# The attention projections of a two-layer kernel as Strassen products over heads, batches and halves of the inputs

## The chip, the cores and the metric

The kernel runs on one core of one Trainium2 chip. A core has five engines that run beside each other and wait for each other by semaphores: PE (TensorE, matmuls; its weight loads are listed as PEld), DVE (VectorE), ACT (ScalarE), POOL (GpSimd) and SP (SyncE, which here only issues DMA transfers). Matmuls read SBUF and write PSUM, which has eight banks of 2 KB per partition. The metric is the device time of one execution in microseconds. Before the change it is 3163.42 us, the median of three runs (3163.29 to 3165.45).

## The reference

Two layers, each an attention-like part times a gated MLP, added to the input; all in float32. Of the first layer, which the change is in:

```python
xn = _layernorm(x, axis=-1)                       # x: 2 x 1024 x 512
q = silu(causal_dwconv(xn @ Wq, qcw, qcb))        # Wq, Wk, Wv, Wg: 512 x 2048, 16 heads of 128
k = silu(causal_dwconv(xn @ Wk, kcw, kcb))        # convolution over 4 tokens
v = silu(causal_dwconv(xn @ Wv, vcw, vcb))
def step(S, ...):                                 # over 1024 tokens, per batch and head
    err = S @ kt - vt
    S = at * S - bt * outer(err, kt)
    ot = S @ qt
o = layernorm(o over the head) * ln_w + ln_b
s = (o * sigmoid(xn @ Wg)) @ Wo
x = x + s * silu(mlp(xn))
```

The second layer has a gated linear recurrence and an MLP with 4-bit weights; the change does not touch its work.

## The kernel before

**Front (0 to 393 us).** x is normalised, transposed and kept in SBUF as `xnT` (128 x 4 x 2 x 1024: input part, batch, token). The first layer's MLP runs step by step on PE; between its steps (`some`, L455) the kernel makes k of head groups 0 to 2 (`for hg in range(3)`, L987). A head group is two heads of both batches, four streams; there are eight groups. k is written to DRAM, as are the decay factors e and the inverses of triangular blocks (`invert`, L746) that the recurrence needs.

**The loop (393 to 1814 us).** The recurrence is done in chunks of 128 tokens. A round u of the loop (L1122) handles one group and one chunk; two groups take turns, so there are 64 rounds of some 22 us, and four rounds cover a window of 256 tokens of two groups. In a round stand `within` (L785, products of one chunk: pk, pqk), `across` (L832, the recurrent chain: pks, pr, zw, pst, with its state), `finish` (L907, output, normalisation, gate), and beside them two pieces of projection. A piece is one of q, k, v, gate for one group and one window. `wide` (L608) makes it: for each of two heads, four matmuls of 512 columns (256 tokens of two batches) over the four parts of the inputs, into one PSUM bank:

```python
lhsT=w[:, kc, hl * P : (hl + 1) * P],
rhs=xnT[:, kc, :, p * 2 * P : (p + 1) * 2 * P],
```

`project` (L624) then copies the sum out (ACT), makes the convolution's last tap out of PSUM (ACT), the other three taps (DVE, six instructions a piece), and silu (ACT). `gated` (L676) takes tanh straight from PSUM. POOL copies the margins of three tokens from window to window (`halo`) and makes kg, qg, rs and the gated output. k of groups 3 to 7 is made in the loop, one piece in each of two rounds of four, followed by `ahead_l` (L725, product pkk).

**Order.** In the loop PE, DVE, ACT and POOL keep the order in which the program records their instructions (`Ordered`, L124). `weave` (L1040) divides a round into ten slots, advances one link of one of two chains in each, and shares out the other products by planned costs. `later(n, ...)` (L593) records a step n slots on; a sum that PE has just finished is thus evicted in the next slot. SP's transfers are in-order on SP's queue: among them the 12 small copies of a round that regroup w into wt (`back`, L876), ground, kb, eb, eg, od. A late instruction on one of these queues delays all behind it.

**PSUM in the loop.** Pool "a" has three banks (pieces, pqk, pkk, half outputs), "i" one (pk), "s" one, "o" one, "z" two.

**After the loop.** `Join` (L140) multiplies the outputs by Wo for each of 16 tiles of 128 tokens, multiplies by the MLP's result, adds x, normalises and transposes for the second layer. For eight tiles (`pd`) the half of the product over the first eight heads is made in late rounds of the loop (`half`) and parked in DRAM. Wo is loaded in rounds 58 to 61 (`load_wo`).

Of the kernel before, what the change touches and what calls it, by code (L numbers as in the profile page):

```python
# [13 lines left out]
F32 = mybir.dt.float32  # L14
# [125 lines left out]
class Join:  # L140
# [5 lines left out]
    def __init__(self, tc, a, cst, minus_half, od, gd, x1d, pd):  # L146
        self.tc, self.a, self.cst, self.minus_half = tc, a, cst, minus_half
        self.od, self.gd, self.x1d, self.pd, self.a = od, gd, x1d, pd, a
        self.ctx = ExitStack()
        self.tp = [self.pool("j_t", 1)]  # L150
        self.wp, self.op = self.pool("j_w", 1), [self.pool("j_o", 1)]
        self.lp = self.pool("j_ln", 3)
        self.wo = []
        self.order = [(c, b) for c in range(NC) for b in range(B)]
        self.o, self.xg, self.made = [], [], 0
        self.load_xg()
# [4 lines left out]
    def load_wo(self):  # L161

        h0 = len(self.wo)
        w = self.wp.tile([P, 4, D], F32, name=f"wo_{h0}")
        self.tc.nc.sync.dma_start(
            w, self.a["wo"][h0 * P : (h0 + 4) * P, :].rearrange("(h p) e -> p h e", p=P)
        )
        self.wo += [w[:, h, :] for h in range(4)]
# [139 lines left out]
def first_layer(ctx, tc, a, cst, minus_half, keep, xnT, od, gd, pd, then):  # L308
# [34 lines left out]
    kp = early.enter_context(tc.tile_pool(name="at_k", bufs=1))  # L343
    dr = ctx.enter_context(tc.tile_pool(name="at_d", bufs=6, space=DRAM))
# [14 lines left out]
    pools["p"] = front.enter_context(  # L359
        tc.tile_pool(name="f0_p", bufs=3, side="right", reuse_waits="tile")  # L360
    )
# [139 lines left out]

    cw = cp.tile([P, 3, H, 4], F32, name="cw")
# [12 lines left out]
    def load_weights(hg, names, queue=nc.sync):  # L515
        w = {}
        for n in names:
            pool = pools["w"] if n != "wk" else kp if "b" in pools or not hg else fz
            w[n] = pool.tile([P, KC, 2 * P], F32, tag=n, name=f"{n}_{hg}")
            queue.dma_start(  # L520
                w[n], a[n][:, hg * 256 : (hg + 1) * 256].rearrange("(kc p) n -> p kc n", p=P)
            )
        return w


# [82 lines left out]
    def wide(name, hg, p, w):  # L608


        for hl in range(2):
            pool, tag = (pools["i"], "pi") if "b" not in pools and hl else (pools["a"], "pa")
            pp = pool.tile([P, B, 2 * P], F32, tag=tag, name=f"{name}_{hl}")
            for kc in range(KC):
                mm(
                    pp,
                    lhsT=w[:, kc, hl * P : (hl + 1) * P],
                    rhs=xnT[:, kc, :, p * 2 * P : (p + 1) * 2 * P],
                    start=(kc == 0),
                    stop=(kc == KC - 1),  # L620
                )
                yield WIDE, (hl, pp) if kc == KC - 1 else None

    def project(j, n, hg, p, w, dst):  # L624

        u = f"{n}_{hg}_{p}"

        def convolved(hl, pp):
            h = hg * 2 + hl
            pre = pools["p"].tile([P, B, 2 * P + 4], F32, tag="pre", name=f"pre{u}_{hl}", bufs=3)  # L630
            acc = dst[:, 2 * hl : 2 * hl + 2, :]

            def first():
                if p == 0:
                    POOL.memset(pre[:, :, 0:3], 0.0)
                else:
                    POOL.tensor_copy(pre[:, :, 0:3], halo[:, j, h % 4, :, 0:3])
                ACT.copy(pre[:, :, 3 : 2 * P + 3], pp)
                ACT.activation(
                    acc, pp, AF.Identity, scale=cw[:, j, h, 3:4], bias=cb[:, j, h : h + 1]  # L640
                )

            def taps(*which):
                for tap in which:
                    DVE.scalar_tensor_tensor(
                        acc,
                        in0=pre[:, :, tap : tap + 2 * P],
                        scalar=cw[:, j, h, tap : tap + 1],
                        in1=acc,
                        op0=ALU.mult,  # L650
                        op1=ALU.add,
                    )

            def second():
                if p < NC // 2 - 1:
                    POOL.tensor_copy(halo[:, j, h % 4, :, 0:3], pre[:, :, 2 * P : 2 * P + 3])
                taps(0, 1)

            def fourth():
                if hl:  # L660
                    ACT.activation(dst, dst, AF.Silu)

            if j == 2 and hg >= HG - 3 and hl:

                later(1, first, lambda: (second(), taps(2)), fourth)
            elif j == 2 and hg >= HG - 3:
                later(1, lambda: (first(), second()), lambda: (taps(2), fourth()))
            else:
                later(1, first, second, lambda: taps(2), fourth)

        for cost, ready in wide(f"p{u}", hg, p, w):
            if ready:
                convolved(*ready)
            yield cost

    def gated(hg, p, w, gate):  # L676
        def act(part, pg):

            ACT.activation(part, pg, AF.Tanh, scale=0.5)
            ACT.activation(part, part, AF.Identity, bias=1.0)  # L680

        for cost, ready in wide(f"pgate_{hg}_{p}", hg, p, w):
            if ready:
                hl, pg = ready
                later(1, functools.partial(act, gate[:, 2 * hl : 2 * hl + 2, :], pg))
            yield cost


    def ahead_k(hg, p, wk, store):
        ka = pa.tile([P, NS, 2 * P], F32, tag="ka", name=f"ka_{hg}_{p}")  # L690
        store["ka", p] = ka
        yield from project(1, "wk", hg, p, wk, ka)
        later(5, lambda: nc.sync.dma_start(store["k"][p], ka))
# [31 lines left out]
    def ahead_l(hg, c, store):  # L725
# [3 lines left out]
        pool, tag = (pools["a"], "pa") if order["loop"] else (pools["i"], "pi")  # L729
        pkk = pool.tile([P, NS, P], F32, tag=tag, name=f"pkk_{hg}_{c}")  # L730
# [54 lines left out]
    def within(hg, c, store):  # L785
# [3 lines left out]
        q = windows[hg, c // 2]["q"][:, :, half]  # L789
# [8 lines left out]
        def block(s):  # L798
# [14 lines left out]
            lambda: POOL.tensor_tensor(qg, q, eg[:, :, 1 : P + 1], ALU.mult),  # L813
# [10 lines left out]
        pqk = pools["a"].tile([P, NS, P], F32, tag="pa", name=f"pqk_{u}")  # L824
# [7 lines left out]
    def across(hg, c):  # L832
# [9 lines left out]
        vv = windows[hg, c // 2]["v"][:, :, half].rearrange("p s (b t) -> p s b t", t=32)  # L842
# [64 lines left out]
    def finish(hg, c):  # L907
# [46 lines left out]
        gate = windows[hg, c // 2]["gate"][:, :, half]  # L954

        def gate_it():
            POOL.tensor_tensor(ot, ot, gate, ALU.mult)
# [20 lines left out]
    def ell():  # L978
        if ls:
            hg, p = ls.pop(0)  # L980
            for c in (2 * p, 2 * p + 1):
                done(ahead_l(hg, c, stores[hg]))
                if c == 2 * p:
                    some(1)

    of_e = ()
    for hg in range(3):  # L987
        stores[hg] = new_store(hg)
        wk = load_weights(hg, ("wk",))
        steps = invert(hg - 1, stores[hg - 1]) if hg else iter(())  # L990
        for p in range(NP):
# [3 lines left out]
            done(ahead_k(hg, p, wk["wk"], stores[hg]))  # L995
# [18 lines left out]
    for n, bufs, at in (("g", 1, ctx), ("b", 2, ctx), ("w", 2, last_w)):  # L1014
# [7 lines left out]
    for n, bufs in (("a", 3), ("i", 1), ("s", 1), ("o", 1), ("z", 2)):  # L1022
# [5 lines left out]
    def made(hg, p, n):  # L1028

        dst = pools["b"].tile([P, NS, 2 * P], F32, tag=n, name=f"{n}_{hg}_{p}")  # L1030
# [733 lines left out]
```

## Time and profile before

| | us |
|---|---|
| median of three runs | 3163.42 |
| span of the profiled execution | 3161.9 |
| PE busy | 3135.2 (99%) |
| DVE busy | 2149.5 (68%) |
| ACT busy | 1253.1 (40%) |
| POOL busy | 826.8 (26%) |
| front / loop / joining / second layer | 392.6 / 1421.7 / 144.8 / 1202.8 |

The profile is of one execution, a few tenths of a per cent at most from the others. A row of a group reads: line, engine, operation, tiles written <- read, shapes, count | busy us, mean ns of one | idle time before. Most rows have line 132, the helper that records the instructions; so groups are told apart by their tiles. A float32 matmul leaves two records, each 0.16 us longer than the step to the next one, since matmuls are pipelined; its cost is therefore taken from start to start.

### The profile page before, as it was taken

The page shows a single profiled execution, that of the slowest core. Times are in us where ns is not written, and L with a number is a line of the kernel's source. Part 1 is how long each engine was busy: PE and PEld are TensorE (multiplying, and loading weights), DVE is VectorE, ACT ScalarE, POOL GpSimd, SP SyncE. Part 2 cuts the span into 40 slices and gives each one's busy share as a digit, 9 for nine tenths or more (in the row PEclk, how much of TensorE's full clock was granted, in tenths as well). Part 3 has the DMA queues.
Part 4 walks back from the last instruction along what each step waited for, and adds up shares of the span by engine and source line. Part 5 has one row for each costly group of instructions (what it writes and reads, how often), then busy time and mean ns, then how long its engine had stood idle before and what let it go on. Part 6 is the DMA issues. An engine that isn't in the chain of part 4 may idle for free.

```text
span 3161.9 us, 38109 instructions
## 1 busy us (share of the span) xinstructions
PE 3135.2 (99%) x12390; PEld 1942.6 (61%) x12390; DVE 2149.5 (68%) x4294; ACT 1253.1 (40%) x2269; POOL 826.8 (26%) x1210
## 2 busy tenths in 40 slices
PE   8999999999999999999999999999999999999998
PEld 7577756666666666666666644555555555555554
DVE  4557678786877878675554455677767666776677
ACT  3476555546555555544333211222222222222223
POOL 2000123223222222322222211333333333333322
PEclk9999999999999999999999999999999999999999
DMA  6244344444444443444324465000101001010014
GB/s 184 63 120 112 102 137 119 109 133 124 126 108 127 140 127 105 107 142 106 89 82 144 118 206 154 29 27 27 33 28 34 27 27 34 27 34 27 27 37 133
DMA packets 499750, 287.40 MB, mean 91 GB/s; under 512 B 207584, under 2 KB 440800, under 8 KB 499552
## 3 DMA queue, kind: packets, MB, share of 16 engines
q1 hardware_dynamic: 490688, 268.97, 30.2%
q0 software_dynamic: 6560, 11.80, 1.3%
q10 hardware_dynamic: 2304, 4.20, 0.4%
q8 instruction: 99, 1.62, 0.2%
q14 instruction: 99, 0.81, 0.1%
HBM read 183.90 MB, written 88.34 MB: 86 GB/s over the span
## 4 chain that ended last, share of the span: by engine, by line
PE 92%; DVE 4%; ACT 1%; issue 1%; DMA 1%; SPq 0%; POOL 0%; DVEq 0%; ACTq 0%; POOLq 0%
PE po L132 18%; PE pua L132 7%; PE pga L132 7%; PE pgate L132 6%; PE pwq L132 6%; PE pwv L132 6%; PE pwk L132 6%; PE zw L132 4%; PE jpo L211 4%; PE puc L132 3%; PE pgc L132 3%; PE pu L132 3%; PE pg L132 3%; PE pr L132 2%; PE pub L132 2%; PE pgb L132 2%
## 5 line engine op out<-in xcount | busy, mean ns | idle before, releaser
L132 DVE TENSOR_TENSOR acc<-acc,po 128x512 f32<-128x512 f32 x408 | 278.1, 682 | 208.4 <-PE po L132 207.7
L132 PEld LDWEIGHTS po<-w_d,i 128*128 128x128 f32 x1024 | 194.5, 190 | 142.6 <-issue 110.7
L132 PE MATMUL po<-w_d,i 128*128 128x256 f32 (+1 forms) x1024 | 275.3, 392 | 0.0
L132 PE MATMUL pgate<-xnT,wg 128*128 128x512 f32 x512 | 245.7, 593 | 0.0
L132 PE MATMUL pwq<-xnT,wq 128*128 128x512 f32 x512 | 245.2, 593 | 0.0
L132 PE MATMUL pwv<-xnT,wv 128*128 128x512 f32 x512 | 243.0, 593 | 1.8 <-ACT gate L132 1.8
L132 PE MATMUL pua<-xq,w_u 128*128 128x512 f32 x512 | 240.6, 592 | 0.0
L132 PE MATMUL pga<-xq,w_g 128*128 128x512 f32 x512 | 240.6, 592 | 0.0
L132 PE MATMUL pwk<-xnT,wk 128*128 128x512 f32 x512 | 236.1, 593 | 1.3 <-ACT ka L132 1.3
L132 ACT COPY g<-pga 128x512 f32<-128x512 f32 x96 | 56.3, 586 | 445.8 <-PE pga L132 438.4
L132 ACT COPY w<-zw 128x128 f32<-128x128 f32 x192 | 50.8, 265 | 368.3 <-PE zw L132 368.2
L132 PEld LDWEIGHTS po<-w_d,s 128*128 128x128 f32 x720 | 136.8, 190 | 95.4 <-issue 77.0
L132 DVE SCALAR_TENSOR_TENSOR v<-prewv,cw,v 128x512 f32<-128x512 f32 x192 | 165.3, 861 | 43.6 <-ACT v L132 35.3
L132 DVE TENSOR_TENSOR rr<-rr,zw 128x128 f32<-128x128 f32 x192 | 54.8, 286 | 205.0 <-PE zw L132 201.4
L132 PE MATMUL po<-w_d,s 128*128 128x256 f32 x720 | 184.8, 379 | 0.0
L132 POOL TENSOR_TENSOR rs<-rs,minus_half 128x4 f32<-128x4 f32 x64 | 64.5, 1008 | 433.1 <-DVE rs L132 415.2
L132 ACT ACT_TABLE_LOAD x133 | 170.6, 1283 | 17.8 <-PE pr L132 11.3
L132 POOL TENSOR_TENSOR ot<-ot,gate 128x512 f32<-128x512 f32 x64 | 85.7, 1340 | 350.2 <-ACT ot L132 320.5
L132 PEld LDWEIGHTS zw<-rr,ground 128*128 128x128 f32 x512 | 97.0, 191 | 122.1 <-issue 102.4
L132 DVE SCALAR_TENSOR_TENSOR ka<-prewk,cw,ka 128x512 f32<-128x512 f32 x192 | 147.7, 771 | 30.2 <-ACT ka L132 25.3
L132 DVE SCALAR_TENSOR_TENSOR q<-prewq,cw,q 128x512 f32<-128x512 f32 x192 | 158.0, 824 | 12.2 <-POOL eg L132 7.0
L132 PEld LDWEIGHTS zw<-w,ground 128*128 128x128 f32 x768 | 110.9, 191 | 64.1 <-issue 53.7
(248 smaller groups left out, 6645.7 us busy)
## 6 DMA issues: line engine op xcount, KB each, us to landing
e<-gr SPq DMA_DIRECT2D x64, 256.0 KB, 4.1
de<-e SPq DMA_DIRECT2D x64, 256.0 KB, 2.7
dk<-ka SPq DMA_DIRECT2D x32, 512.0 KB, 2.8
kb<-dk SPq DMA_DIRECT2D x64, 256.0 KB, 3.4
eg<-egr SPq DMA_DIRECT2D x64, 256.0 KB, 4.0
eb<-de SPq DMA_DIRECT2D x64, 256.0 KB, 3.4
od<-ot SPq DMA_DIRECT2D x64, 256.0 KB, 2.2
wt<-w SPq DMA_DIRECT2D x768, 16.0 KB, 1.9
```

The costliest lines, as they stand in the source:

```text
L132: i = getattr(self.engine, name)(*args, **kw)
L211: matmul(po, lhsT=ot[:, h, :], rhs=self.wo[h], start=(h == h0), stop=(h == H - 1))
```

## The change

A piece is no longer a plain product. It is seen as a product of 2 x 2 blocks: two heads (rows), two halves of the 512 inputs (inner), two batches (columns). By Strassen's scheme in Winograd's form the eight block products become seven; each is two matmuls of 256 columns (`quarter`), 14 for a piece. The operands are sums: three weight blocks and three x blocks more, plus two changed in place, so a set is seven blocks.

- x sums: made once per window in the front by POOL (`x_sums`) and written to DRAM (`dx`); in the loop the seven blocks of a window are loaded into the room of `xnT` itself (`load_x`, two windows at a time; `boths` has the rest of that room), every fourth round.
- weight sums: for each weight and group made once by POOL after loading (`load_w`, p = 0), written to DRAM (`dw`) and reloaded for each further window. Four buffers of a set; two sets are loaded each round.
- a piece (`Piece.step`): products 0, 5, 6, 3 add up in one bank (A), which ACT copies out after each; products 1 and 4 go to a second bank (X), from which one ACT copy takes both; product 2 adds to X, and DVE adds it out of PSUM. POOL (before round 48) or DVE adds the pair to the outer quarters. Then come convolution and silu, or tanh, out of SBUF, in more slots than before. The copy that fed the convolution's last tap from PSUM is replaced by one from SBUF.
- two pieces of a round are interleaved in a fixed order of steps (`ORDER`, `woven`), and the pieces of the four turns are redistributed (`tasks`): k and gate; v and k; q and gate; q and v.
- PSUM: "a" has two banks, "x" one; pkk and pqk move to "i", which has one.
- k of group 3 moves to the front, where k pieces are made with plain products (`direct`); the loop makes k of groups 4 to 7. The first q and v pieces of groups 0 and 1 are made ahead of the loop, with their loads and sums on POOL's queue.
- eleven halves of the output product instead of eight (`pd`); Wo goes to xnT's room in round 62.

Core of the diff:

```diff
-    def wide(name, hg, p, w):
-        for hl in range(2):
-            pool, tag = (pools["i"], "pi") if "b" not in pools and hl else (pools["a"], "pa")
-            pp = pool.tile([P, B, 2 * P], F32, tag=tag, name=f"{name}_{hl}")
-            for kc in range(KC):
-                mm(pp, lhsT=w[:, kc, hl * P : (hl + 1) * P],
-                    rhs=xnT[:, kc, :, p * 2 * P : (p + 1) * 2 * P], ...)
+    def quarter(out, w, x, i, first):
+        for kc in range(2):
+            mm(out, lhsT=w[:, i, kc, :], rhs=x[:, i, kc, :],
+                start=(first and kc == 0), stop=(kc == 1), skip_group_check=not first)
...
+        def step(self, i):
+            out = self.out
+            if i in (0, 5, 6, 3):
+                for step in self.of_a:
+                    step()
+                self.of_a = []
+                quarter(self.A, self.w, self.x, i, i == 0)
+                at = {0: 0, 5: 1, 6: 3, 3: 2}[i]
+                def copied():
+                    ACT.copy(out[:, at], self.A)
+                    ...
+                self.evicted(self.of_a, copied)
+            elif i == 1:
+                self.X = pools["x"].tile([P, 2, 2 * P], F32, tag="X", name=f"px{self.u}")
+                quarter(self.X[:, 0], self.w, self.x, 1, True)
+            elif i == 4:
+                quarter(self.X[:, 1], self.w, self.x, 4, True)
+                def pair():
+                    ACT.copy(self.both, self.X)
+                    self.end()
+                self.evicted(self.of_x, pair)
+            else:
+                for step in self.of_x:
+                    step()
+                quarter(self.X[:, 1], self.w, self.x, 2, False)
+                def add():
+                    DVE.tensor_tensor(out[:, 1], out[:, 1], self.X[:, 1], ALU.add)
+                    self.ended()
+                later(1, add)
...
-        pkk = pool.tile([P, NS, P], F32, tag=tag, name=f"pkk_{hg}_{c}")
+        pkk = pools["i"].tile([P, NS, P], F32, tag="pi", name=f"pkk_{hg}_{c}")
...
-        pqk = pools["a"].tile([P, NS, P], F32, tag="pa", name=f"pqk_{u}")
+        pqk = pools["i"].tile([P, NS, P], F32, tag="pi", name=f"pqk_{u}")
...
-    for hg in range(3):
+    for hg in range(4):
...
-    for n, bufs in (("a", 3), ("i", 1), ("s", 1), ("o", 1), ("z", 2)):
+    for n, bufs in (("a", 2), ("x", 1), ("i", 1), ("s", 1), ("o", 1), ("z", 2)):
...
+    def load_w(n, hg, p, queue):
+        w = pools["w"].tile([P, 7, 2, P], F32, tag="w", name=f"w{n}_{hg}_{p}")
+        if p:
+            return [
+                lambda: queue.dma_start(w[:, 0:4], dw[n, hg][:, 0:4]),
+                lambda: queue.dma_start(w[:, 4:7], dw[n, hg][:, 4:7]),
+            ], [], []
+        ...
+            lambda: POOL.tensor_tensor(s1, a21, a22, ALU.add),
+            lambda: POOL.tensor_tensor(s2, s1, a11, ALU.subtract),
+            lambda: POOL.tensor_tensor(s4, a12, s2, ALU.subtract),
+            lambda: POOL.tensor_tensor(a21, a11, a21, ALU.subtract),
+        ], [lambda: queue.dma_start(dw[n, hg], w)]
...
+    ORDER = (
+        (0, 0), (1, 0), (0, 1), (0, 4), (0, 5), (1, 5), (0, 2),
+        (0, 6), (1, 6), (1, 1), (1, 4), (0, 3), (1, 3), (1, 2),
+    )
...
+            for i, t in enumerate(tasks(u + 1)):
+                loads, sums, kept = load_w(*t, nc.sync)
+                later(2 + 2 * i, *loads)
+                later(5 + 2 * i, lambda sums=sums: [step() for step in sums])
+                later(9, *kept)
+            if turn4 == 3 and u // 4 + 2 < 4 * NP:
+                later(1, *load_x(u // 4 + 2, nc.sync))
...
-    pd = {i: tc.dram_tile([P, D], F32, name=f"pd_{i}") for i in (4, 5, 7, 8, 10, 11, 12, 13)}
+    pd = {i: tc.dram_tile([P, D], F32, name=f"pd_{i}") for i in range(3, 14)}
```

## The prediction

> **What bounds the kernel now.** I read the page first, then the busy time by stage, the chain and PE's waits, then eight rounds of the loop, and last single rows. Part 1 and the chain of the page:
>
> ```profile
> PE 3135.2 (99%) x12390; PEld 1942.6 (61%) x12390; DVE 2149.5 (68%) x4294; ACT 1253.1 (40%) x2269; POOL 826.8 (26%) x1210
> PE 92%; DVE 4%; ACT 1%; issue 1%; DMA 1%; SPq 0%; POOL 0%; DVEq 0%; ACTq 0%; POOLq 0%
> ```
>
> TensorE is busy 99% and is 92% of the chain: only 27 us of the span are not matmuls. So work taken from PE is time gained, as long as nothing else becomes late. PE's waits inside the loop say how late the others are now (PE's waits, 392.6 to 1814.3 us):
>
> ```profile
> PE pst L132 <- DVE wt L132: 1.9, 2, 1.7
> PE pwv L132 <- ACT gate L132: 1.8, 3, 0.6
> PE zw L132 <- ACT w L132: 1.7, 5, 0.5
> ```
>
> A few us in 1422: nothing is late. The stages (front, rounds up to 32, later rounds, joining, second layer), then single rounds; columns are stretch, length, busy us of PE, PEld, DVE, ACT, POOL, clock, DMA share, GB/s:
>
> ```profile
> 392.60:1149.20 756.60, 753.93 (x3591) 484.05 (x3591) 579.23 (x1359) 417.09 (x832) 205.72 (x396) 1.00 0.46 125
> 1149.20:1814.30 665.10, 660.81 (x3194) 429.58 (x3193) 409.02 (x1073) 284.61 (x596) 173.79 (x273) 1.00 0.41 112
> ...
> 449.80:472.60 22.80, 22.80 (x115) 15.00 (x114) 19.85 (x47) 11.92 (x23) 5.55 (x12) 1.00 0.36 103
> 472.60:496.50 23.90, 23.31 (x116) 15.22 (x115) 19.06 (x44) 14.65 (x31) 7.40 (x13) 1.00 0.37 98
> 496.50:519.10 22.60, 22.23 (x106) 14.04 (x105) 21.53 (x51) 9.83 (x20) 6.44 (x15) 1.00 0.35 93
> 519.10:541.10 22.00, 22.00 (x107) 14.02 (x107) 18.55 (x48) 12.21 (x27) 7.10 (x13) 1.00 0.38 116
> ```
>
> The second engine is DVE: 79.0 us in these four rounds of 91.3. In the round where it is at 95% PE already lost 0.4 us. The clock is 1.00, so it plays no part.
>
> **The change part by part.** *Products.* A piece (one of q, k, v, gate for two heads and 256 tokens of both batches) is 8 matmuls of 512 columns now and 14 of 256 afterwards. A matmul has two records here. What 256 columns cost is seen in the second layer (PE's timeline):
>
> ```profile
> 2205.09 1.02 PE L132 MATMUL puc<-xq,w_u 128*128 128x512 f32 x2
> 2205.95 1.03 PE L132 MATMUL po<-w_d,s 128*128 128x256 f32 x4
> 2206.81 1.02 PE L132 MATMUL pga<-xq,w_g 128*128 128x512 f32 x2
> ```
>
> From start to start one matmul of 512 columns takes 0.86 us and two of 256 take 0.86: half the columns are half the time, with a new weight load each. A piece goes from 6.88 to 6.02 us. Of 128 pieces 112 change (the 16 k pieces of head groups 0 to 3 are made in the front in the old way): 112 x 0.86 = **-96.3 us**, all on the path.
>
> *Moved.* k of group 3 goes from loop to front, and three more half output products (11 for 8) from the joining into late rounds; the same matmuls, 0. Cover: DVE in the front is 239 of 393 us, in the late rounds 409 of 665. If the cover were gone, four k pieces' taps (24 x 0.77 us) would be the cost.
>
> *Transition to the loop.* Now PE runs from the front into the first product without a gap (PE's timeline at 392.63 us). Afterwards the x sums are read back into xnT's own room, so 7 of 14 loads must wait for the last direct k matmul, on POOL's queue. About 12 us of PE work stand between (21 records of the MLP's last product at 0.235, three pkk at 0.9, more). Behind the waiting load on POOL are six weight loads, the 3.3 us clearing of the ground, and 16 weight sums before the first four pieces, 8 more before round 0. POOL's issue row is 0.75 us; a 128x256 sum takes 0.79 to 0.83; so a weight set costs POOL 2 x 0.75 + 4 x 0.8 + 0.75 = 5.5 us against 6.0 of PE, plus landings of 6.7 us. I work out that PE stands some 3 us for wk's and 2 for gate's sums, and put 2 for the start: **+7**. Ends: 0 (all covered) and 25 (the loads of 1.8 MB land one behind the other, as uwT and dwT did at 9 and 11.4 us).
>
> *DVE.* Each piece adds one add of 128x256 out of PSUM; neighbours are 286 ns (128x128, rr) and 682 ns (128x512, kd), I take 0.42. POOL gets a 128x512 add per piece (its rows are 1.27 to 1.40 us) while the round is below 48. POOL's work slows DVE's taps: 137 of v's 192 taps meet no POOL tensor instruction and take 749 ns, the nine wholly beneath one take 1268 on average. In the trace:
>
> ```profile
> 507.11 2.45 DVE L132 SCALAR_TENSOR_TENSOR v<-prewv,cw,v 128x512 f32<-128x512 f32 x2
> ...
> 507.29 1.73 POOL L132 TENSOR_TENSOR kg<-kb,eg 128x512 f32<-128x512 f32 x1
> ```
>
> Two taps that take 1.5 us alone took 2.45. Summed over q, v, ka and the inversion's tl and ml this excess is 73 us, against 310 us of POOL's large work: 0.24 us per us. Per round POOL gains 2 x 1.34, so DVE gains 0.64 + 0.84. Four rounds: 79.0 + 3.4 + 2.6 = 85.0, against PE's 91.3 - 6.9 = 84.4. DVE is then as full as PE. Worse, the new order puts v and k pieces in one round (turn 1), whose 12 taps fall mostly in one stretch: I count 24.7 us of DVE in rounds 1, 9, 17, 25 against PE's 21.1, and 17.5 in the next. Late next: the add that frees the single X bank, and kd, lt, at, which now share one PSUM bank (pi) where three banks served; PE returns to it about 3.8 us later, so about 1 us of lateness is free. 2.6 us in such a round and 1.4 in round 3 of 8: **+16** over four such eights. Ends: 0 (the order's slack covers 3.6 us) and 60 (DVE late in every one of the 32 rounds by 2).
>
> [...]
>
> *ACT.* A piece's evictions become four copies of 128x256 and one of 128x512, from two of 128x512; the scaled copy then reads SBUF. Rows: 265 ns at 128x128, 586 at 128x512, I take 0.40: +1.0 us for q, k, v, and +1.8 for gate (two of 128x1024 at 1.06 for four of 0.62). The instruction order of the changed kernel has 38 more table loads, all in rounds up to 30, because tanh, silu and exp now alternate more:
>
> ```profile
> L132 ACT ACT_TABLE_LOAD x32 | 41.1, 1283 | 0.5
> ```
>
> 38 x 1.283 = 49 us of ACT, 1.5 per round. The fullest rounds (5, 13, ..) come to 20.9 of 22: covered, 0, with at most the 0.6 us of the longest ACT wait now at each such round.
>
> [...]
>
> *Queues.* SP issues 26 transfers a round at 0.55 us, 14.3 us. Added are four weight loads per round (0.42 to 0.46 each) and seven of x sums every fourth: by rows the two rounds after these hold 43 to 45 us of issues in 42. Behind them wait the wt copies (12 a round), needed some 10 us after their slot and landing in 1.9. The bytes: 2 x 0.92 + 0.46 MB a round are 109 GB/s beside 125 at a share of 0.46; at the same rate the share becomes 0.86. On 12 rounds POOL carries 3.2 or 6.4 us of weight sums and waits for their landing, ahead of kg and rs. I put **+10** for these; ends 0 and 40 (3 us in 13 rounds).
>
> *Joining.* Half products follow each other eleven times, where four did; there the DMA share was 0.95 at 288 GB/s, and 4 MB of wo move into rounds 62 and 63. **+2**, ends 0 and 15.
>
> Sum: -96.3 + 7 + 16 + 10 + 2 = -61.3. The profiled execution's span is 3161.9 us; 3100.6 follows. The median of the three runs, 3163.4, lies 1.5 above that span, so I say **3102**.
>
> **The rivals.** *All is covered.* PE's waits now are 6 us in the loop, which speaks for it; DVE at 85.0 of 84.4 against it. 3163.4 - 96.3 + 2 to 12 = 3069 to 3080.
>
> *DVE or SP becomes the bound of the first 32 rounds.* For: the sums above, where both reach PE's new time. Against: the late half has room (61%). With DVE's and the queues' ends, 60 + 40, most of the gain is gone: 3125 to 3157.
>
> *Slower: PE stands at each hand-over of the accumulating bank.* The new piece returns to bank A three times and to X once while ACT must first copy the earlier sum, and DVE frees X: five hand-overs a piece, where there were two with a bank to spare. At 0.17 us each, 112 x 5 x 0.17 = 96, the gain is gone; at 0.3 it is 3163 + 72 = 3235. Now such a wait reaches 0.6 us, in three cases. Against it: two or more other steps, 2 to 3 us, lie between the returns, and a copy takes 0.4.
>
> **How the numbers follow.** My forecast (3080 to 3125) 0.52; all covered 0.16; bound of DVE or SP 0.20; slower 0.10; no difference beyond 0.2% (6 us, about what a measurement of this kernel can tell) 0.02. Faster 0.88, same 0.02, slower 0.10. The range leaves out the slower case and the ends of the others: 3072 to 3145.
>
> **What would show it.** Right: rows of 14 x 2 records of 128x256 per piece, and PE's busy time near 3040; rounds 2 to 32 of about 21 us, with waits of PE on DVE (kd, lt, at, X's add) in every eighth round, few beyond round 32; a gap of 5 to 10 us near 420 us. Wrong: waits of PE on ACT's copies out of bank A in most rounds, 256-column matmuls further apart than 0.43 us, or SP's transfers landing so late that PE waits for wt or G.

## The result and the profile after

The changed kernel takes 3376.57 us (median; 3373.87 to 3379.14) beside 3164.28 us before (four runs made beside it): a ratio of 1.0673, 95% interval 1.0658 to 1.0688. It is 212 us slower; 61 us faster was forecast, and the time lies far outside the range. The direction is that of the third rival, to which the forecast gave 0.10, but not for its reason, as will be seen.

Part 1 of the page after, its row of granted clock and the chain:

```profile
PE 3132.9 (93%) x13734; PEld 2245.8 (67%) x13734; DVE 2207.3 (65%) x4429; ACT 1416.7 (42%) x2646; POOL 1051.3 (31%) x1304
...
PEclk9999989999889999999999999999999999999999
...
PE 37%; DVE 0%; DMA 0%; issue 0%; POOL 0%; ACT 0%; SPq 0%; ACTq 0%; DVEq 0%; POOLq 0%
```

PE's busy time is the same as before (3132.9, was 3135.2), although 95 us of matmuls were taken out. Busy time counts a matmul at half clock as nearly twice as long (four records of 128x256 took 1.92 us at 665.64 us, where the clock was 0.50, and 1.03 at 656.60, where it was 1.00), so the saving has been eaten inside the busy time as well; the 8s in the clock's row say where. The chain can't be followed through the loop any more, so the waits have to be read instead. PE's waits in the loop (523 to 2010 us), in total, times, longest:

```profile
PE pk L132 <- DMA kb<-dk: 61.9, 18, 7.7
PE pqk L132 <- DVE kd L132: 58.9, 34, 4.6
PE pxq L132 <- ACT xnT L132: 16.3, 9, 3.2
PE paq L132 <- ACT preq L132: 12.6, 12, 3.1
PE pak L132 <- ACT prek L132: 12.1, 6, 3.7
PE pkk L132 <- DVE at L132: 9.1, 7, 3.4
```

Before, the longest rows were 1.9, 1.8 and 1.7 us. Now there are 18 stops for a load (kb), some fifty for DVE and as many for ACT. The second row needs care: pqk does not read kd. It is computed from kb and q; what it waits for is the bank pi, which kd still has to read. And kd is often late because it needs eb, which has not landed: this holds for 18 of the 34 stops and 38 of the 59 us. DVE's own row of waits in the loop, and one case by the timelines of DVE and PE:

```profile
DVE kd L132 <- DMA eb<-de: 115.0, 23, 13.5
```

```profile
893.24 0.69 DVE L132 TENSOR_TENSOR kd<-pk,eb 128x512 f32<-128x512 f32 x1 [12.91 <-DMA eb<-de]
```

```profile
893.99 1.16 PE L132 MATMUL pqk<-q,kb 128*128 128x128 f32 x8 [2.21 <-DVE kd L132]
```

(xnT in the third row is the room in which `both` lies, the copy of X.)

Stages by windows (transition, first 32 rounds, later rounds, joining; columns as in the prediction):

```profile
436.60:523.10 86.50, 69.03 (x317) 56.05 (x316) 45.50 (x71) 41.02 (x84) 52.75 (x79) 0.90 0.72 231
523.10:1362.70 839.60, 694.88 (x4113) 620.98 (x4112) 561.95 (x1356) 479.11 (x985) 295.01 (x383) 0.94 0.61 182
1362.70:2008.90 646.20, 595.26 (x3499) 509.96 (x3498) 400.53 (x1061) 294.01 (x656) 211.26 (x253) 0.97 0.61 179
2008.90:2169.60 160.70, 159.48 (x470) 78.94 (x469) 88.71 (x223) 18.70 (x38) 26.56 (x33) 1.00 0.63 197
```

DVE has 562 us of work in 840: it is no bound by load. To separate the three things that make PE late, I counted each matmul record at what it takes at full clock (0.43 us for 512 columns, 0.215 for 256, 0.11 for 128, from start to start in the timelines), the time in which no matmul ran, and half of the time at clock 0.5:

| us, before → after | length | work | idle | lost to the clock |
|---|---|---|---|---|
| front and transition | 449.8 → 523.1 | 430.9 → 465.6 | 11.2 → 34.4 | 0 → 11.9 |
| rounds up to 32 | 699.4 → 839.6 | 694.0 → 635.0 | 2.7 → 144.7 | 0 → 51.2 |
| later rounds | 629.4 → 646.2 | 620.2 → 570.4 | 4.3 → 50.9 | 1.7 → 17.1 |
| joining | 180.5 → 160.7 | 180.3 → 159.0 | 0 → 1.2 | 0 → 0 |
| second layer | 1202.8 → 1205.4 | 1193.4 → 1193.4 | 8.5 → 10.9 | 2.5 → 3.5 |
| sum | 3161.9 → 3375.1 | 3118.8 → 3023.4 | 26.7 → 242.1 | 4.2 → 83.7 |

The work fell by 95.4 us, as computed (96.3). Against it stand 215 us more of standing still, 80 us of half clock and 14 of small remainders. The question is why PE stands.

### The profile page after: what moved, and what is told of

Read it like the earlier page. It is cut to its first block, busy times and chain, and to the rows that moved or that the text cites. A ratio compares the mean times of both kernels' runs of the same rounds, so it can differ in the third digit from the quotient of the medians.

```text
span 3375.1 us, 41994 instructions
## 1 busy us (share of the span) xinstructions
PE 3132.9 (93%) x13734; PEld 2245.8 (67%) x13734; DVE 2207.3 (65%) x4429; ACT 1416.7 (42%) x2646; POOL 1051.3 (31%) x1304
## 5 line engine op out<-in xcount | busy, mean ns | idle before, releaser
L132 ACT ACT_TABLE_LOAD x171 | 219.4, 1283 | 19.3 <-PE pr L132 11.3
L132 POOL TENSOR_TENSOR rs<-rs,minus_half 128x4 f32<-128x4 f32 x64 | 82.5, 1290 | 384.0 <-DVE rs L132 376.7
L132 PEld LDWEIGHTS po<-w_d,s 128*128 128x128 f32 x720 | 136.8, 190 | 95.4 <-issue 77.0
L132 DVE SCALAR_TENSOR_TENSOR ka<-prek,cw,ka 128x512 f32<-128x512 f32 x192 | 152.1, 795 | 35.8 <-ACT ka L132 31.9
L132 DVE SCALAR_TENSOR_TENSOR v<-prev,cw,v 128x512 f32<-128x512 f32 x192 | 168.9, 882 | 5.5 <-ACT v L132 4.2
L132 ACT ACTIVATE on<-po,nm,rs 128x128 f32<-128x128 f32 x256 | 103.9, 462 | 113.9 <-DVE nm L132 113.8
L132 PE MATMUL paq<-xnT,wq 128*128 128x256 f32 x512 | 137.6, 392 | 13.0 <-ACT preq L132 13.0
L132 PE MATMUL pav<-xnT,wv 128*128 128x256 f32 x512 | 141.2, 400 | 7.7 <-ACT prev L132 7.7
L132 DVE SCALAR_TENSOR_TENSOR q<-preq,cw,q 128x512 f32<-128x512 f32 x192 | 143.5, 764 | 5.9 <-ACT q L132 3.7
L132 PEld LDWEIGHTS pua<-xq,w_u 128*128 128x128 f32 x512 | 96.0, 190 | 76.8 <-issue 72.2
L132 PEld LDWEIGHTS pga<-xq,w_g 128*128 128x128 f32 x512 | 97.2, 190 | 72.9 <-issue 66.7
L132 PE MATMUL pagate<-xnT,wgate 128*128 128x256 f32 x512 | 138.7, 395 | 4.2 <-ACT prev L132 2.3
```

The lines of the kernel that those rows point to most:

```text
L132: i = getattr(self.engine, name)(*args, **kw)
```

## The experiments

Three theories were in play. "Place": pk and pqk, and with them kb, eb and q, are wanted much earlier in the round than before (at about 41% and 59% of PE's planned work, once 85% and 100%). "Loads": the reloads fill the DMA engines and SP's queue, so kb and eb land late. "Hand-overs": PE returns to banks that ACT or DVE has not yet emptied; this splits into the accumulating banks A and X (the forecast's rival) and, later, the bank pi.

**Place, bytes and queue, one at a time.** pk behind the third fifth of the products and pqk behind the last:

```
             products(1)
+            products(2)
             other(ready, 1, 4 * TURN)
-            products(2)
-            other(ready, None, 4 * NARROW)
             products(3)
             ell(1)
             products(4)
+            other(ready, None, 4 * NARROW)
```

> The changed kernel with pk one fifth of a round later (from 41% to 57% of the round's planned PE work) and pqk at the end of the round (from 59%). Theory 'place' (pk and pqk stand too early for the loads of kb and eb, which are issued from the round's start on): PE's waits for kb and for kd, 120 us together, fall under 30, the clock loss in the loop falls from 68 us to under 40, and the time from 3377 to 3200 to 3270. Theory 'bytes' (the reloads fill the DMA engines) and theory 'issues' (SP's queue is too long): the lateness shows at other waits (wt, ground, eg) and the time stays at 3320 or more.

Measured: 3349.03 us (ratio 1.0585, 1.0554 to 1.0615), 28 us better, where "place" had expected 3200 to 3270. kb's wait fell from 62 to 13 us and pqk's on kd went, but PE's waits in the loop after it read:

```profile
PE pxq L132 <- ACT xnT L132: 53.8, 19, 5.4
PE pkk L132 <- DVE kd L132: 23.0, 11, 3.4
PE pav L132 <- ACT prev L132: 19.6, 10, 3.6
```

X's copy, 16 us before, now cost 54. At 540 us, for instance, ACT had stood 5.5 us in `on` for DVE's nm, with the copy of X behind it in ACT's order.

The same move alone, made in the kernel before (pk and pqk at 37% and 58% in rounds 0 to 39):

```
+            other(lead, 6, 6 * WIDE)
+            other(ready, 1, 4 * TURN)
+            other(lead, None, 2 * WIDE)
...
+            other(ready, None, 4 * NARROW)
...
```

(the second piece's products stand in three parts around ready's last step and ell(0))

> The kernel before with pk and pqk at 37% and 58% of the planned PE work in rounds 0 to 39 (from some 85% and 100%), nothing else changed. Theory 'place': PE waits for kb or kd by 50 us or more, the clock falls after such waits, and the time rises by 60 to 150 us to 3220 to 3310. Theories 'bytes' and 'issues': without the reloads nothing is late, 3164 to 3190.

Measured: 3189.59 us (1.0081, 1.0052 to 1.0110). In this kernel the early place costs 25 us, less than "place" had expected (60 to 150), and not by late loads. Two of PE's rows of waits:

```profile
PE zw L132 <- ACT w L132: 18.1, 18, 2.1
```

```profile
PE pk L132 <- DMA kb<-dk: 4.6, 2, 2.7
```

kb was issued 10 us or more before pk in 27 of the rounds 1 to 31. So the early place alone does not make PE wait for kb, and that late_pk gained about as much (28 us) is no confirmation: there other waits went than came here.

Fewer bytes: the reloads bring 16 of 128 partitions, into four fixed weight tiles (the operands are mostly stale; the issues stay).

```
-            lambda: queue.dma_start(w[:, 0:4], dw[n, hg][:, 0:4]),
+            lambda: queue.dma_start(w[0:16, 0:4], dw[n, hg][0:16, 0:4]),
```

> The changed kernel with every reload of a weight set and of x sums cut to 16 of 128 partitions (an eighth of the bytes, the same number of transfers), so that its products use stale operands. Theory 'bytes': landings of kb, eg and eb fall back from 4.7, 6.7 and 7.4 us to about 3.6, 4.2 and 3.7, and the time to 3200 to 3260. Theory 'issues': landings fall, but issues stay late; the time stays above 3320. Theory 'place': eb lands 3 us earlier, so kd's wait falls by about half, kb's by a quarter: 3290 to 3340.

Measured: 3329.47 us (1.0523, 1.0488 to 1.0558): 47 us, not the 3200 to 3260 expected if the bytes alone were the cause. The median landing of eb in the first 32 rounds went from 7.7 to 5.1 us, kb's from 4.7 to 3.6.

The reloads issued on ACT's queue (`load_w(*t, nc.scalar)` and `load_x(.., nc.scalar)` for `nc.sync`):

> The changed kernel with the loop's reloads (four a round, seven more each fourth round) issued on ACT's queue instead of SP's. Theory 'issues': SP is as free as before the change, kb and eb are issued 3 us earlier, the time falls to 3230 to 3290. Theory 'bytes': no gain, 3350 or more. Theory 'place': kb's and kd's waits fall by about a third where SP was late, and ACT, which issues at 0.4 us each, gets 2.5 us a round more: 3300 to 3400.

Measured: 3373.31 us (1.0661, 1.0631 to 1.0692), nothing gained. kb's wait fell to 18 us, the wait for X's copy rose to 70. The issue times say what made kb late: in the changed kernel it was issued 4.0 to 6.1 us before pk in rounds 5 to 31, hardly more than its landing takes (4.7 us in the median), where the kernel before has 9 us or more. With the reloads on ACT's queue it was again 10 us or more in 27 of the rounds 1 to 31. So it was SP's queue that brought kb late; with the queue relieved, PE stood for ACT instead.

**The accumulating banks.** The copies between products read a constant, in the same places of ACT's order:

```
+    still = cst[:, 0:2, :].rearrange("p k t -> p (k t)")
...
-                    ACT.copy(out[:, at], self.A)
+                    ACT.copy(out[:, at], self.A if i == 3 else still)
-                    ACT.copy(self.both, self.X)
+                    ACT.copy(self.both, still.unsqueeze(1).to_broadcast([P, 2, 2 * P]))
```

> The changed kernel, but the copies that stand between a piece's products (three of bank A's four, and bank X's pair) read a constant in SBUF instead of the bank: ACT has the same instructions at the same places, and PE no longer waits for them (the pieces' values are left out). 'Hand-overs' (PE stands because ACT, in its own order, has not yet copied a bank): PE's waits on ACT for paq, pxq, pak, pav, pxgate (52 us in the loop) go, and with them their share of the clock loss, 20 to 50 us: 3270 to 3310. 'Loads' (PE stands because kb lands late, and because DVE stands for eb): those 120 us stay, the ACT waits were only the next in line: 3330 to 3376.

Measured: 3372.55 us (1.0656, 1.0625 to 1.0687), the changed kernel's time. Nearly all of the waits on ACT were gone, and PE's waits in the loop were:

```profile
PE pqk L132 <- DVE kd L132: 106.0, 43, 5.7
PE pk L132 <- DMA kb<-dk: 73.6, 22, 7.9
```

PE stood some 50 us less for ACT and some 55 us more for kb and for pi. So the rival's mechanism exists, but taking it away alone gives nothing. The "loads" theory expected just this, but its own remedies come next.

**The loads.** Stores by the queue of the engine that made the data, so that SP does not stand in front of later loads:

```
-            nc.sync.dma_start(od[c][:, hg * NS : (hg + 1) * NS, :], ot)
+            nc.gpsimd.dma_start(od[c][:, hg * NS : (hg + 1) * NS, :], ot)
-            later(1, lambda: nc.sync.dma_start(store["k"][p], ka))
+            queue = nc.scalar if order["loop"] else nc.sync
+            later(1, lambda: queue.dma_start(store["k"][p], ka))
```

(and the same for the store of e)

> The changed kernel, but the stores of od go out from POOL's queue and those of dk and de from ACT's queue, from the engine that made them, so that SP no longer waits for POOL's ot (78 us), ACT's ka (67 us) and e ahead of the loads behind them. 'Loads': kb and eb are issued earlier; PE's waits for kb and kd (120 us) fall below 40, and the clock loss with them: 3240 to 3300. 'Hand-overs': as when the reloads went to another queue, the ACT waits take their place, and ACT now issues 1.5 transfers a round as well: 3340 to 3390.

Measured: 3355.57 us (1.0602, 1.0571 to 1.0633): 21 us, where "loads" had expected 3240 to 3300. And a second buffer for eb (`bufs=1` to `bufs=2`, kg in exchange):

> The changed kernel with a second buffer for eb (room for it from kg, which goes from two buffers to one). With one buffer the load of eb can't start before at of the round before is made, and SP stands in front of everything behind it. 'Loads': DVE's wait for eb in kd (115 us) and PE's wait for kd behind it (59 us) mostly go: 3290 to 3330. 'Next in line': as in the four earlier changes to the order and the queues, half or less of it: 3340 to 3370.

Measured: 3378.50 us (1.0681, 1.0620 to 1.0741): nothing, less than either expectation. kd still waited 130 us for eb; the buffer was not what held it.

**Remedies together.** late_pk, own_queues and `on` one place later in ACT's order:

```
-            lambda: (centred(), normed(0, 1)), lambda: normed(2, 3),
+            centred, lambda: normed(0, 1), lambda: normed(2, 3),
```

> Three remedies in one: pk and pqk at the end of the round's products, stores from the makers' queues, and ACT's normalization (on) one place later in its order, so that ACT does not stand for DVE's nm (102 us in the loop) with the banks' copies behind it. If the stops have these three causes and no others, PE's idle time in the loop falls below 80 us and the time to 3180 to 3230. If each remedy only uncovers the next late hand-over: 3290 to 3340, with ACT's copies of X still the longest wait.

Measured: 3294.38 us (1.0409, 1.0379 to 1.0439): 82 us, more than late_pk and own_queues apart (28 + 21; `on` alone was not tried). 128 us of idle time and 37 of clock were left in the loop. Then a second bank for X with the products in an order that returns to every bank four products later (the bank comes from putting both chains' zw into one):

```
-        (0, 0), (1, 0), (0, 1), (0, 4), (0, 5), (1, 5), (0, 2),
-        (0, 6), (1, 6), (1, 1), (1, 4), (0, 3), (1, 3), (1, 2),
+        (0, 0), (1, 0), (0, 1), (0, 4), (0, 5), (1, 5), (1, 1),
+        (1, 4), (0, 6), (1, 6), (0, 2), (1, 2), (0, 3), (1, 3),
```

> The kernel with the three remedies (pk and pqk late, makers' queues, on one place later) and a second bank for X (both chains' zw in one bank), with the 14 products reordered so that every return to a bank comes four products later, X's for the second piece four and for the first seven. PE's waits for ACT's copies of X (30 us there) and for A (14 us) should go: 3240 to 3265. If other hand-overs take their place, 3280 to 3300.

> As x_two, with the second buffer for eb as well. PE's wait on kd (29 us) goes too; idle time in the loop 50 to 80 us and less than 20 us lost to the clock: 3190 to 3240. Below 3160 only if the transition's 20 us and the front's 8 were gone as well, which it does not touch.

Measured: 3294.86 us (1.0416, 1.0386 to 1.0446) and 3291.32 us (1.0405, 1.0375 to 1.0435). Both had been expected to gain. X's waits (31 us) went and nothing was gained: kb's rose from 10 to 35, and 28 us of waits at zw are new, where both chains now share a bank.

**What a stop costs.** The kernel before with one controlled stop in each of 32 rounds:

```
+            turn(pot[:, 0, :], on[:, 0, :])
+            ACT.copy(ot[:, 0, :], pot[:, 0, :])
+            for i in range(5):
+                ACT.copy(ot[:, (i + 1) % 2, :], ot[:, i % 2, :])
+            turn(pot[:, 1, :], ot[:, 1, :])
```

> The kernel before, with one stop of PE put into each of the rounds 1 to 32: between the transposes of on, PE waits for a chain of six short copies on ACT (some 2 us). It measures what a stop costs by itself. 'Clock' (a stop of over 1 us also halves the clock for some 3.4 us): 32 x 2 us idle and 32 x 1.7 us lost to the clock, 3164 + 64 + 55, 3260 to 3330, and a stretch of clock 0.5 after nearly every stop. 'Idle only': 3164 + 64, 3220 to 3240, clock 1.00.

Measured: 3265.43 us (1.0317, 1.0274 to 1.0361), 100.2 us more. PE's longest row of waits, and a stretch with one stop and the half clock behind it (columns as above, the clock third from the end):

```profile
PE pot L132 <- ACT ot L132: 65.5, 32, 2.5
```

```profile
470.00:495.00 25.00, 24.76 (x114) 16.38 (x113) 16.36 (x40) 12.86 (x29) 5.74 (x10) 0.93 0.30 77
```

Of 32 stops of 2.0 us, 20 were followed by 3.41 us at clock 0.5: 65.5 + 20 x 3.41 x 0.5 = 99.6. The profiled run is the slower of the two (3271.19 us, 106 more than the kernel before); the rest of its difference is about the 64 added transposes, 64 x 0.11 = 7.0. So a stop of 2 us cost 3.1 on average. The other 12 stops had no such stretch behind them.

**Is it Strassen's products at all?** Plain products (8 matmuls of 512 columns from xnT, raw weights, two evictions) in rounds 0 to 31 or 0 to 23, Strassen's pieces after that with the three remedies. The x sums in the front, the half products and the set of PSUM banks are the changed kernel's; in the plain rounds pkk and pk share pi, and pqk has X's bank:

```
+                for kc in range(KC):
+                    mm(
+                        pp,
+                        lhsT=w[:, (0, 1, 3, 2)[2 * hl + kc // 2], kc % 2, :],
+                        rhs=xnT[:, kc, :, self.p * 2 * P : (self.p + 1) * 2 * P],
+                        start=(kc == 0),
+                        stop=(kc == KC - 1),
+                    )
...
+            if u < SWITCH:
+                pieces = [piece(*t).plain(weights.pop(t), t[0] == "q") for t in sorted(now, key=lambda t: t[0] == "v")]
```

> Rounds 0 to 31 make q, k, v and gate by plain products from xnT (8 matmuls of 512 columns, raw weights, two evictions, the order of the kernel before); the x sums and weights' sums are loaded and Strassen's pieces run from round 32 on, with pk and pqk late, stores from the makers' queues and on one place later. What else the change does (x sums in the front, k a slot ahead, half products, one shared bank pi) stays. In late_own_on the rounds after 32 and the joining took 772 us against 810 before. 'Short slack between hand-overs, where DVE, ACT and SP are full': the first 32 rounds return to some 700 us, the later ones keep their gain, less 10 to 15 us where the sums are loaded at round 32 and 5 to 10 in the front: 3140 to 3155, faster than before. If the rest of the change (the shared bank pi, the front) is itself what stops PE: over 3180.

> The same with Strassen's pieces from round 24 on. Eight more rounds save 8 x 1.7 us of PE work, and lose, at late_own_on's (103 + 29) us in 32 rounds, some 33 us: by 'short slack' 15 to 25 us slower than half_way.

Measured: 3280.79 us (1.0366, 1.0350 to 1.0381) and 3299.63 us (1.0424, 1.0407 to 1.0442). Strassen's pieces in rounds 24 to 31 are thus 19 us slower than plain products there. But the surprise is the first number: with plain products the first 32 rounds still took 788 us, against 699 in the kernel before, for 8 us less of work. PE's waits in them:

```profile
PE pk L132 <- issue: 48.0, 16, 4.3
PE pkk L132 <- DVE kd L132: 14.2, 14, 1.7
```

The first row names no releaser, but in all 16 cases pk starts 0.1 us after a DVE lt ends: it waits until lt has read pkk out of pi. The kernel before has three turning banks for the pieces, pkk and pqk, and pi for pk alone. The change gives one of the three to X and puts pkk, pk and pqk on pi; in these plain rounds it is pkk and pk that meet there, and the pieces have two banks. So the banks of before, for the same plain rounds:

```
+    bank = itertools.cycle("aax")
...
+        n = next(bank)
+        return pools[n].tile(shape, F32, tag="A" if n == "a" else "X", name=name)
...
-        pkk = pools["i"].tile([P, NS, P], F32, tag="pi", name=f"pkk_{hg}_{c}")
+        pkk = turned([P, NS, P], f"pkk_{hg}_{c}")
```

(and so for pqk, which was in X's bank, and the pieces' halves)

> As half_way, but in rounds 0 to 31 the pieces' halves, pkk and pqk take turns over three banks (A, A and X's) and pk has pi alone, as in the kernel before. In half_way pk waits 47 us there for pi, which DVE's lt has not yet read (its waits have no releaser in the list; pk starts 0.1 us after lt ends). 'Bank budget' (pkk, pk and pqk on the one bank pi are the change's own cost, with plain products as with Strassen's): those waits, pkk's on kd (14 us) and the clock behind them (24 us) go, rounds 0 to 31 come near 715 us from 788, and the time to 3195 to 3215. 'Other causes' (kb's landing, the reloads of weights): 3250 to 3280.

Measured: 3213.44 us (1.0149, 1.0132 to 1.0166), 67 us better; the 32 rounds took 724. Two things differ here at once: pkk leaves pi, and the pieces have a third bank to turn over. Next, the sharing by itself, in the kernel before, which keeps its three banks for the pieces (the first pkk and pk come two products earlier, and two products stand ahead of pqk):

```
-        pqk = pools["a"].tile([P, NS, P], F32, tag="pa", name=f"pqk_{u}")
+        pqk = pools["i"].tile([P, NS, P], F32, tag="pi", name=f"pqk_{u}")
```

(and so for pkk)

> The kernel before, with only pkk and pqk moved to the bank pi of pk (the pieces keep three banks; to leave room between the three users, the first pkk and pk come two products earlier and the last two products stand ahead of pqk). 'Bank budget': DVE's backlog of 3 to 7 us in the rounds with pkk now reaches PE, as in half_way against half_way_banks (67 us): 3200 to 3240, with PE's waits on DVE's lt and kd. If the bank alone is harmless without the change's other parts: 3160 to 3175.

Measured: 3334.22 us (1.0535, 1.0504 to 1.0565): 169 us, twice and more what was expected, from no added work, no added bytes and no products of Strassen's. PE's waits in this kernel:

```profile
PE pk L132 <- issue: 54.0, 20, 3.7
PE pqk L132 <- DVE kd L132: 45.2, 23, 4.1
PE pqk L132 <- DVE lt L132: 13.8, 10, 1.9
```

In the first row, too, pk starts 0.1 us after an lt ends, in all 20 cases. The three rows are 113 of the 122 us for which PE stands in this loop (7 in the kernel before); another 51 go to the clock. No wait here is for a load, and the two moved products are not taken apart from the bank.

One case, by the timelines of PE and DVE:

```profile
464.35 1.05 PE L132 MATMUL pkk<-ka 128*128 128x128 f32 x8
...
471.07 1.09 PE L132 MATMUL pk<-cst,kb 128*128 128x128 f32 x4 [3.72 <-issue]
...
473.23 3.62 PE L132 MATMUL pgate<-xnT,wg 128*128 128x512 f32 x4
```

```profile
466.89 1.20 DVE L132 COPY wt<-zw 32x128 f32<-32x128 f32 x4
468.12 0.69 DVE L132 TENSOR_TENSOR e<-e,cst 128x512 f32<-128x512 f32 x1
468.73 1.53 DVE L132 SCALAR_TENSOR_TENSOR q<-prewq,cw,q 128x512 f32<-128x512 f32 x2
470.27 0.69 DVE L132 TENSOR_TENSOR lt<-pkk,e 128x512 f32<-128x512 f32 x1
```

pkk is complete at 465.4 and lt, which takes 0.69 us, begins at 470.27: DVE was busy all that time with what stands ahead of it. In the kernel before, with a bank to spare, PE's list has no wait of pk or pqk at all; here pk waits 3.7 us for lt, and the two matmuls of pgate (four records) take 3.62 us instead of 1.88, at half clock.

The reverse, a second bank for pi under Strassen's pieces (from zw, as above), alone and on late_own_on:

> The changed kernel with a second bank for pi (from zw, both chains' zw in one bank) and nothing else. PE's wait of pqk on kd (59 us in the loop) is a wait for the bank, not for kd's values: pqk reads kb and q alone, and takes pi when kd has read pk out of it. 'Bank budget': it goes, with pkk's on at (9 us) and their clock loss; new waits of zw take 10 to 28 us back: 3290 to 3330. 'Next in line' (kb's landing, 62 us, and ACT's copies grow as in free_banks): 3350 to 3380.

> late_own_on (Strassen's pieces throughout, the three remedies, 3294 us) with a second bank for pi, taken from zw (both chains' zw in one bank, which in x_two cost 28 us of new waits between zw, pst and wt). 'Bank budget': pkk's wait on kd (29 us) and pk's for lt go, and DVE's backlog no longer reaches PE there; against it the zw waits: 3255 to 3285. 'Next in line': 3290 to 3310.

Measured: 3360.04 us (1.0616, 1.0586 to 1.0647) and 3281.15 us (1.0370, 1.0349 to 1.0391), 17 and 13 us better, the second with intervals that just overlap. In the first pqk's wait on kd is gone, but 37 us of new zw waits came with the packed bank, and kb's wait and ACT's copies stayed.

What follows from all of these: PE stands at much the same points of the round for several causes that lie behind each other, kb's and eb's landing, pi, and ACT's copies of A and X. Taking one away lengthens the waits for others (late_pk, act_queue, free_banks, x_two). Put alone into the kernel before, the shared pi costs 169 us and the early place 25. These prices are not shares of the 212: the pi that costs 169 waits for lt and for kd in DVE's order, while in the changed kernel 38 of the 73 us for pi lie behind eb's landing, and a second bank for pi gained 17 us there. How the 212 us divide among the causes is not shown. No version reached the kernel before; the best with Strassen's pieces, half_way_banks, is 50 us slower than it. There, the part ahead of the loop takes 506 us against 450 (some 42 of it matmuls, k of group 3 and others moved out of the loop); rounds from 32 on and the joining together take 783 us for 729 of work, against 810 for 801 before. What remains there was not taken apart further.

## Why the prediction was wrong, point by point

The step that failed is the price of the other engines' lateness. The sum allowed 35 us for all waits of PE (7 + 16 + 10 + 2) and nothing for ACT or for the clock. PE stood 215 us longer than before, and the clock took 80 more. The saving in products came as computed.

- **Products**, -96.3: right, -95.4 by count at full clock. Four records of 128x256 take 1.03 us in the loop where the clock is full, as two of 128x512 do (1.02 before), so half the columns are half the time.
- **"The clock is 1.00, so it plays no part"**: a term put at nothing. It was 1.00 in a loop in which PE stood for 7 us in all. It was not a constant to be read off but a second price on stops: each us of added standing came with 0.37 us of clock (80 beside 215).
- **The move of pk and pqk** within the round has no term in the sum. In before_early it costs 25 us.
- **DVE**, +16 (0 to 60): the right place was named ("kd, lt, at, which now share one PSUM bank (pi) where three banks served"), and sized wrongly. The working compared DVE's load with PE's time per round and allowed 1 us of lateness. The load was not the matter (562 us in 840). PE's waits on DVE for pi in the changed kernel come to 73 us (kd 58.9, at 9.1, lt 2.6, ml 2.4). 38 of them lie behind a kd that stood for eb, up to 13.5 us at a time, so they belong as much to the next term; for the others kd was late in DVE's order. That the work ahead of one instruction in DVE's order suffices is shown by before_pi (4.9 us at the lt shown above).
- **Queues**, +10 (0 to 40): 62 us of waits for kb and the 38 behind eb, with the clock behind them. That bytes matter is shown (47 us in few_bytes), and that SP's queue does (own_queues 21 us; kb's issue times in act_queue). The step named wt as what would be late; it was kb and eb. eb was needed 6 to 10 us after its issue in rounds 5 to 31, about its landing time of 7.7, where the kernel before has 10 to 19.
- **Transition**, +7 (0 to 25): 17.5 us idle and 8.5 of half clock between front and loop, 26 together, just beyond the upper end; the front itself has 5.7 more idle and 3.4 of clock.
- **ACT**, 0: some 50 us of PE's waits are on ACT, whose copies stood behind `on`, which waits for nm. free_banks shows that taking these waits away alone gains nothing. The 38 more table loads came (171, was 133, 1283 ns each), and no run tested them alone.
- **Joining**, +2: right; 160.7 us for 159.0 of work.
- **The rival "DVE or SP becomes the bound of the first 32 rounds"**, 0.20: DVE was not full (562 us in 840), but SP's queue did bring kb and eb late. Its range does not follow from its terms: both ends, 60 + 40, with -96.3, 7 and 2 give 3176, not 3157 at most.
- **The rival "slower: PE stands at each hand-over of the accumulating bank"** said 3235 at 0.3 us per hand-over. PE does stand at hand-overs, but its waits for pi (73 us) are longer than those for A and X (some 50), and the argument against it ("2 to 3 us lie between the returns, and a copy takes 0.4") compared with the copy's duration, not with its place in ACT's order. The chance of 0.10 rested on that.
- **Signs**: of those listed for "wrong", waits of PE on ACT's copies appeared (32 stops for bank A in 64 rounds); wt and G late did not. Rounds 0 to 31 took 26 us each, not 21. Busy time near 3040 was listed for "right" and could not have appeared with the clock falling.

## What to carry to other kernels

When a change takes a PSUM bank, list every user of each bank with the instruction that empties it, and compare the distance to the next user with the work that stands ahead of that instruction in its engine's order, not with its duration or the engine's load. Follow a late instruction one step further back: a bank that DVE empties late may be waiting for a load. Price a stop of a saturated PE with its clock: stops of 2 us cost 3.1 each here. And when the slack is gone in several places, removing one wait proves little; put the suspected one alone into the kernel that has slack, as before_pi and before_early do, and look at which waits it brings before its price is carried back.

## What the runs showed of the hardware

Not expected: after how short a stop the clock fell, and that its length alone did not decide it. In the loops of stops, before_pi and the changed kernel together, of 55 stops of 0.3 to 0.9 us one lay in a stretch at 0.5 or within 3.4 us ahead of one; of 53 between 0.9 and 1.9 us, eight; of 58 between 1.9 and 2.6 us, 33; of 41 longer ones, 37. In the changed kernel alone these were one of 49, three of 27, seven of 12 and 20 of 24. So the "over 1 us" in the expectation of stops was the author's estimate, and the runs did not bear it out: most stops of 0.9 to 1.9 us had no half clock with them or behind them, nor had 12 of the 32 controlled ones of 2.0 us.

In the loop of the changed kernel the clock was 0.5 in 29 stretches: 19 of 3.41 us, nine of 6.83 and one of 10.24. The loop of the kernel before has one, of 3.41 us at 1323.9 us, after a stop of 1.7 us.
